# Layer 0 with its engines held to the traced order of instructions, a fourth e buffer, strip borders from ScalarE, and six groups ahead of the transposes

## The chip, the cores and the metric

The kernel runs on one core of a Trainium2 chip. The metric is device time in microseconds for one execution, and less is better. Times without a profiler come from several executions, of which the median is given. The profile comes from one execution of its own. Five engines matter: PE (TensorE, matrix products), DVE (VectorE), ACT (ScalarE), POOL (GpSimd) and SP (SyncE, which here issues nearly all DMAs). Each runs its own list of instructions from the front to the back, and engines wait for each other through semaphores.

## The reference

The input x has 4 images of 16 channels and 256 x 256 pixels. Two layers follow each other, and each adds its result to its input.

```
x = x + L0(_gn(x))     # _gn: normalization over 8 groups of 2 channels
x = x + L1(_gn(x))

# L0: a 3x3 convolution gives 16*25 logits for each pixel
out     = conv(x, conv_w) + conv_b
weights = softmax(out.reshape(N, C, 25, H, W), axis=2)
L0      = einsum('ncuij,ncuij->ncij', unfold5x5(x), weights)

# L1: a 3x3 convolution of silu(x) and of 8 cubic B-splines of x
L1      = einsum(silu(patches), base_w) + einsum(bspl(patches), spl_w) + bias
```

Layer 0 is the part that the change is about. For each pixel and channel it forms 25 exponentials, sums them, sums their products with the 5 x 5 neighbourhood, and divides the second sum by the first.

## The kernel before

The program is written with tiles and pools. A scheduler in the framework gives each engine its order of instructions: it goes by the order in which the code issued them (the traced order), but may put one ahead of another when it expects its operands earlier. Semaphores follow from the order that it settles on.

**Three stages.** The first reads x, gathers the statistics of the groups, builds the weights and normalizes image 0. The second is layer 0. It is written twice, with and without a shift of the logits, and a branch on `flag` picks one at run time; the traces here ran the one without. The third is layer 1. Nothing of one stage's instructions is mixed with those of the next.

**Layer 0's loops.** An image is cut into two halves of 128 rows, which lie on the 128 partitions, and each half into 8 strips of 32 columns: 64 strips in all for four images. A strip is worked in 8 groups of 4 columns (JG = 4), so there are 512 groups. The groups of a strip are counted here from 0 to 7. For one group:

- PE computes the 400 logits of each of 4 columns, in two products each: L544 with the operand am (from the scratch hst) and L548 with an (from hsl, the rounded value and its residue). The result lies in PSUM tiles lg of two columns, of which there are three.
- ACT takes the exponential of two columns at a time into `e[:, 0]` (L567).
- POOL multiplies all four columns by the neighbourhood u and writes `e[:, 1]` (L572).
- DVE sums both halves of e over the 25 neighbours into nd (L481).

The tile e is held from the first exponential to the end of the reduction. Its tag has `bufs=LAG + 2`, which is 3.

**The end of a strip.** The function `sums` runs one group late (LAG = 1): group k's reduction is issued after group k's successor has issued its product. With the last group of a strip it also calls `finish`: DVE takes the reciprocal of the denominators (L490), POOL multiplies by it (L491, "the division") and adds into xc, the held pixels of x (L494). With every fourth strip xc is complete: DVE takes bn_stats of it (L498), and a store of xc to x1s is queued.

**The next image.** While image b is worked, a generator `normalize(b + 1)` prepares the next one. The loop calls `next(ahead)` once in each group, so each `yield` in it stands for one group. For each four channels (q) and each half (h), ACT writes the normalized pixels in two arrangements: hsp (L205, rows with the borders of the strips, stored to hs and later read as u) and ht (L213, for transposing). The outer borders of hsp are zeroed by two memsets on POOL (L218, L219). Two groups later PE transposes ht (L237) into PSUM; after two more, ACT copies the result to tt (L244 to L246) and rounds it to hi (L248); after two more, DVE takes the residue lo = tt - hi (L252); after two more, SP stores tt, hi and lo to hst and hsl (L262, six DMAs). ACT's work on hsp and ht needs xp, the pixels of the next image, which SP loads (L184). Image 3 has no next one, so its strips are free of all this.

**SP's queue.** SP issues the loads of am and an (L439, L449; three buffers), u (L463; two), xc (L469), xp, and the stores. Each waits in its place for the buffer that it fills or for the data that it writes.

Of the kernel before, what the change touches and what calls it, by code (L numbers as in the profile page):

```python
# [9 lines left out]
F32 = mybir.dt.float32  # L10
# [20 lines left out]
def conv_preact_kernel(  # L31
# [12 lines left out]
    nc = tc.nc  # L44
    B, C, H, W = x.shape
    G = 8
    GC = C // G
    P = 128
    NH = H // P
    K = 5  # L50
    KK = K * K
    NL = C * KK
    PAD = K // 2
# [3 lines left out]
    SW = 32  # L57
    NST = W // SW
# [3 lines left out]
    JG = 4  # L62
    LAG = 1
    RP = P + 2
    CT = (W + 2) * RP
    QC = 4
# [9 lines left out]
    const = ctx.enter_context(tc.tile_pool(name="const", bufs=1))  # L76
# [87 lines left out]
    zero = const.tile([PAD * C, max(RP, NST * SP)], F32, name="zero")  # L164
    nc.vector.memset(zero, 0.0)

    def normalize(b, held=None):

        for e in (0, HP - PAD):
            for r in range(PAD):  # L170
                nc.sync.dma_start(
                    hs[b][:, e + r].rearrange("s c w -> c s w"),
                    zero[0:C, 0 : NST * SP].rearrange("c (s w) -> c s w", s=NST),
                )
        for h in range(NH):
            for w in (0, (W + 1) * RP):
                nc.sync.dma_start(hst[b][h][:, w : w + RP], zero[0:C, 0:RP])
                nc.sync.dma_start(
                    hsl[b][h][:, :, w : w + RP].rearrange("c t r -> (c t) r"), zero[:, 0:RP]
                )  # L180

        def load(q):
            for h in range(NH):
                nc.sync.dma_start(  # L184
                    xps[q % 2][h][:, :, PAD : PAD + W],
                    x[b, q * QC : (q + 1) * QC, h * P : (h + 1) * P, :].rearrange(
                        "c p w -> p c w"),
                )

        if held is None:  # L190
            load(0)
        yield
        for q in range(C // QC):
            if held is None and q + 1 < C // QC:
                load(q + 1)
            hts = []
            for h in range(NH):
                xp = xps[q % 2][h] if held is None else held[h][:, q * QC : (q + 1) * QC]
                hsp = prep.tile([P, NST, QC, SP], F32, name=f"hsp{b}_{q}_{h}", tag="hsp")
                ht = prep.tile([P, QW, W // QW, QC], F32, name=f"ht{b}_{q}_{h}", tag="ht")  # L200
                for k in range(QC // GC):
                    g = q * (QC // GC) + k
                    kc = slice(k * GC, (k + 1) * GC)
                    how = dict(scale=nrm[b][:, 0, g : g + 1], bias=nrm[b][:, 1, g : g + 1])
                    nc.scalar.activation(  # L205
                        hsp[:, :, kc, :].rearrange("p s c w -> p c s w"),
                        bass.AP(
                            tensor=xp.tensor, offset=xp.offset + k * GC * (W + 2 * PAD),
                            ap=[xp.ap[0], [W + 2 * PAD, GC], [SW, NST], [1, SP]],
                        ),  # L210
                        AF.Identity, **how,
                    )
                    nc.scalar.activation(  # L213
                        ht[:, :, :, kc].rearrange("p g w c -> p c w g"),
                        xp[:, kc, PAD : PAD + W].rearrange("p c (w g) -> p c w g", g=QW),
                        AF.Identity, **how,
                    )
                nc.gpsimd.memset(hsp[:, 0, :, 0:PAD], 0.0)  # L218
                nc.gpsimd.memset(hsp[:, NST - 1, :, PAD + SW :], 0.0)  # L219
                hts.append(ht)  # L220
                yield
                yield
                r0 = PAD + h * P
                nc.sync.dma_start(
                    hs[b][:, r0 : r0 + P, q * QC : (q + 1) * QC, :].rearrange(
                        "s r c w -> r s (c w)"),
                    hsp.rearrange("p s c w -> p s (c w)"),
                )
            yield
            yield  # L230
            for n, g0 in enumerate(range(0, QW, QG)):
                tt = tts[n % 2]
                tp = []
                for h in range(NH):
                    t = ptr.tile([P, QG, P], F32, name=f"tp{b}_{q}_{g0}_{h}", tag=f"tp{h}")
                    for k in range(QG):
                        nc.tensor.transpose(  # L237
                            t[:, k, :], hts[h][:, g0 + k].rearrange("p w c -> p (w c)"), ident
                        )
                    tp.append(t)  # L240
                yield
                yield
                for h in range(NH):
                    nc.scalar.copy(tt[:, h, :, 1 : 1 + P], tp[h])  # L244
                nc.scalar.copy(tt[:, 0, :, RP - 1 :], tp[1][:, :, 0:1])
                nc.scalar.copy(tt[:, 1, :, 0:1], tp[0][:, :, P - 1 :])  # L246
                hi = prep.tile([P, NH, QG, RP], F32R, name=f"hi{b}_{q}_{g0}", tag="hi")
                nc.scalar.copy(hi, tt)  # L248
                yield
                yield  # L250
                lo = prep.tile([P, NH, QG, RP], F32R, name=f"lo{b}_{q}_{g0}", tag="lo")
                nc.vector.tensor_sub(lo, tt, hi.bitcast(F32))  # L252
                yield
                yield
                for h in range(NH):

                    o = q * QC * CT + (1 + g0) * RP
                    for to, ti, t in ((hst, 0, tt), (hsl, 0, hi), (hsl, 1, lo)):
                        d = to[b][h]
                        m = 2 if to is hsl else 1  # L260
                        t = t if t.dtype == F32 else t.bitcast(F32)
                        nc.sync.dma_start(  # L262
                            bass.AP(
                                tensor=d.tensor,
                                offset=d.offset + q * QC * m * CT + ti * CT + (1 + g0) * RP,
                                ap=[[QW * RP, W // QW], [m * CT, QC], [1, QG * RP]],
                            ),
                            t[:, h].rearrange("p g r -> p (g r)"),
                        )
                yield  # L270


    with tc.tile_pool(name="pre", bufs=1) as pre, tc.tile_pool(
        name="xin", bufs=2
    ) as xin, tc.tile_pool(name="stat", bufs=2) as stat, tc.tile_pool(
        name="pstat", bufs=1, space=PSUM
# [51 lines left out]
        for b in range(B):  # L328
            st = stat.tile([P, G, NH * (GC if b == 0 else 1), 6], F32, name=f"st0_{b}", tag=f"st0{min(b, 1)}")
            for hf in range(NH):  # L330
                n = b * NH + hf
# [27 lines left out]
            if b == 0:  # L359
                ahead = normalize(0, held)  # L360
                next(ahead)
# [51 lines left out]
        for r in range(RT):  # L413
# [4 lines left out]
                ws[r * C : (r + 3) * C, :, r, :], wb1.rearrange("p (e o) -> p e o", e=3)  # L418
            )


    def layer0(shift):

        arm = "g" if shift else ""
        with tc.tile_pool(name=f"im{arm}", bufs=NIM) as imp, tc.tile_pool(
            name=f"l0{arm}", bufs=2
        ) as l0, tc.tile_pool(name=f"plog{arm}", bufs=3, space=PSUM) as plog:
# [38 lines left out]
            def load_xc(n):  # L466
                b, hf, s = strips[n]
                xc = l0.tile([P, C, CX], F32, name=f"xc_{n}{arm}", tag="xc")
                nc.sync.dma_start(  # L469
                    xc, x[b, :, hf * P : (hf + 1) * P, s * SW : s * SW + CX].rearrange(  # L470
                        "c p w -> p c w")
                )
                return xc
# [36 lines left out]
            for n, (b, hf, s) in enumerate(strips):  # L510
                if (hf, s) == (0, 0):
                    for _ in ahead:
                        pass
                    ahead = normalize(b + 1) if b + 1 < B else iter(())
                last = (hf, s) == (NH - 1, NST - 1)
# [8 lines left out]
                for j in range(0, SW, JG):  # L524
# [7 lines left out]
                    if j == SW // 2:  # L532
# [3 lines left out]
                            us.append(load_u(n + 1))  # L536
                        if s * SW % CX == SW and n + CX // SW - 1 < len(strips):
                            nxc = load_xc(n + CX // SW - 1)
                    e = l0.tile([P, 2, JG, K, C, K], F32, name=f"e_{n}_{j}{arm}", tag="e", bufs=LAG + 2)
                    for j1 in range(0, JG, 2):  # L540
                        lg = plog.tile([P, 2, 512], F32, name=f"lg_{n}_{j}_{j1}{arm}", tag="lg")
                        for i in range(2):
# [39 lines left out]
                sums()  # L582
            for o, i in stores:
                nc.sync.dma_start(o, i)

    fast = nc.values_load(
        flag[0:1, 0:1], min_val=0, max_val=1,
# [2 lines left out]
    with tc.If(fast > 0) as small_logits:  # L590
        layer0(False)
    with small_logits.Else():
        layer0(True)
# [3 lines left out]
    with tc.tile_pool(name="l1", bufs=2) as l1, tc.tile_pool(  # L597
        name="stat1", bufs=2
    ) as stat, tc.tile_pool(name="pstat1", bufs=1, space=PSUM) as pstat, tc.tile_pool(
        name="py", bufs=4, space=PSUM  # L600
# [106 lines left out]
        for n, (b, u) in enumerate(units):  # L707
# [3 lines left out]
            f, g = fb[n % 3], sl[n % 2]  # L711
# [89 lines left out]
```

## Time and profile before

| What | Value |
|---|---|
| median of 3 executions | 3744.49 us (3737.02 to 3744.62) |
| the profiled execution | 3743.14 us; span from first to last instruction 3741.2 us |
| mean granted TensorE clock | 0.937 |
| PE busy | 3136.8 us, 84% of the span |
| DVE busy | 3235.6 us, 86% |
| ACT busy | 2053.7 us, 55% |
| POOL busy | 2010.9 us, 54% |
| first and last reciprocal of layer 0 (DVE, L490) start | 204.74 and 2443.42 us |

The span is what the trace covers; the profiled execution's own time is 1.9 us longer, and it lies 1.4 us below the median. The page gives for each group of instructions its busy time, the mean duration of one, and the idle time of its engine just before, with what ended that idle time. The timeline lists single instructions, or runs of equal ones, with start and duration. Matmul ends are modelled, so a busy PE isn't PE at its peak.

### The profile page before, as it was taken

Reading aid. Unit: us, or ns where it says so; the run is one execution under the profiler, and the core shown is the slowest. Engines: PE = TensorE matmul, PEld = TensorE weight load, DVE = VectorE, ACT = ScalarE, POOL = GpSimd, SP = SyncE. Lnnn points to the kernel's source line nnn. Section 1 sums busy time; section 2 is a strip of 40 time slices with the busy share of each in tenths; the row PEclk is TensorE's granted clock in tenths of the full one; section 3 lists DMA queues with packets and bytes.
Section 4 is the critical chain, followed back from the end, with each engine's and each line's share of the span. In section 5 each row is a group of like instructions: output and inputs, shape, how many; then the busy total and the mean of one; then the engine's idle time right before and its main releaser. Section 6 shows DMA issues by size and latency. Waiting matters only on the chain. (4 is left out here: it accounts for less than half of the span.)

```text
span 3741.2 us, 34115 instructions
## 1 busy us (share of the span) xinstructions
PE 3136.8 (84%) x11824; PEld 1696.2 (45%) x11824; DVE 3235.6 (86%) x1627; ACT 2053.7 (55%) x1903; POOL 2010.9 (54%) x750
## 2 busy tenths in 40 slices
PE   1488888978779878779889889849998999998999
PEld 0255555555455545445555555513333433642333
DVE  9488899989899979899989989978788888888886
ACT  3454433454434355434334334358788888888884
POOL 1287888977889879789889989910000000000000
PEclk9999999989899989899989989969999999999999
DMA  7877575567576567665555555467687667667662
GB/s 238 254 213 205 164 198 162 148 177 214 161 202 173 152 185 200 189 194 162 162 157 160 145 156 161 109 134 168 165 177 176 171 172 176 168 168 176 169 168 78
DMA packets 361880, 646.08 MB, mean 173 GB/s; under 512 B 44402, under 2 KB 231140, under 8 KB 353508
## 3 DMA queue, kind: packets, MB, share of 16 engines
q1 hardware_dynamic: 351908, 626.90, 63.7%
q10 hardware_dynamic: 9792, 16.91, 1.4%
q8 instruction: 97, 1.59, 0.2%
q14 instruction: 83, 0.68, 0.1%
HBM read 522.34 MB, written 104.24 MB: 167 GB/s over the span
## 5 line engine op out<-in xcount | busy, mean ns | idle before, releaser
L544 PE MATMUL lg<-wm,am 128*128 128x400 f32 x4096 | 1758.9, 527 | 307.8 <-ACT e L567 283.0
L481 DVE TENSOR_REDUCE nd<-e 128x128 f32<-128x3200 f32 x512 | 1764.6, 3476 | 236.9 <-POOL e L572 153.5
L572 POOL TENSOR_TENSOR e<-e,u 128x1600 f32<-128x1600 f32 x512 | 1797.4, 3543 | 200.2 <-ACT e L567 170.5
L567 ACT ACTIVATE e<-lg 128x800 f32<-128x800 f32 x1024 | 838.1, 837 | 1331.5 <-DVE nd L481 664.3
L548 PE MATMUL lg<-wn,an 97*128 97x400 f32 x2048 | 1167.6, 605 | 0.0
L544 PEld LDWEIGHTS lg<-wm,am 128*128 128x128 f32 x4096 | 794.7, 200 | 670.2 <-ACT e L567 403.4
L742 PE MATMUL yp<-f,wt 128*64 128x512 f32 x4608 | 1031.3, 595 | 35.9 <-DVE f L640 22.6
L742 PEld LDWEIGHTS yp<-f,wt 128*64 128x64 f32 x4608 | 391.1, 136 | 653.2 <-issue 564.3
L680 POOL MEMSET sx<- 96x1024 f32 x8 | 8.5, 1065 | 1220.1 <-ACT sl L713 1213.9
L548 PEld LDWEIGHTS lg<-wn,an 97*128 97x128 f32 x2048 | 402.2, 196 | 324.0 <-issue 40.7
L634 ACT ACTIVATE r<-xt 128x2048 f32<-128x2048 f32 (+2 forms) x128 | 243.3, 1902 | 157.8 <-PE yp L742 32.3
L637 DVE TENSOR_SCALAR xt<-xt 128x2048 f32<-128x2048 f32 (+2 forms) x128 | 156.6, 1224 | 183.2 <-ACT s L635 183.2
L727 ACT ACTIVATE xt<-xt,qs 128x2048 f32<-128x2048 f32 (+2 forms) x128 | 264.9, 2081 | 57.7 <-DMA sx<-x1s 31.6
L638 DVE TENSOR_TENSOR s<-s,xt 128x2048 f32<-128x2048 f32 (+2 forms) x128 | 292.9, 2288 | 2.1
L639 DVE TENSOR_TENSOR s<-s,r 128x2048 f32<-128x2048 f32 (+2 forms) x128 | 292.5, 2285 | 2.6 <-ACT s L636 2.6
L640 DVE TENSOR_TENSOR f<-s,s 128x2048 f32<-128x2048 f32 (+2 forms) x128 | 288.7, 2286 | 0.8
L635 ACT ACTIVATE s<-xt 128x2048 f32<-128x2048 f32 (+2 forms) x128 | 242.5, 1895 | 2.7 <-DVE f L640 2.7
L636 ACT ACTIVATE s<-r 128x2048 f32<-128x2048 f32 (+2 forms) x128 | 242.7, 1896 | 0.0
L750 PE MATMUL yp<-sl,ws 96*64 96x512 f32 x768 | 204.8, 614 | 43.3 <-DMA sl<-zrow 27.3
L490 DVE RECIPROCAL nd<-nd 128x512 f32<-128x512 f32 x64 | 214.6, 3353 | 2.2
L237 PE MATMUL tp<-ident,ht 128*128 128x128 f32 x256 | 57.8, 385 | 124.1 <-ACT ht L213 81.0
L491 POOL TENSOR_TENSOR nd<-nd 128x512 f32<-128x512 f32 x64 | 81.8, 1278 | 143.2 <-DVE nd L490 142.2
(127 smaller groups left out, 843.0 us busy)
## 6 DMA issues: line engine op xcount, KB each, us to landing
xt<-x1s SPq DMA_DIRECT2D x56, 2048.0 KB
am<-hst SPq DMA_DIRECT2D x512, 194.6 KB
u<-hs SPq DMA_DIRECT2D x320, 288.0 KB
an<-hsl SPq DMA_DIRECT2D x512, 129.8 KB
am<-hst SPq DMA_DIRECT2D x256, 129.8 KB
sx<-x1s SPq DMA_DIRECT2D x224, 96.0 KB
hs<-hsp SPq DMA_DIRECT2D x32, 576.0 KB
hst<-tt SPq DMA_DIRECT2D x64, 260.0 KB
```

The costliest lines, as they stand in the source:

```text
L481: nc.vector.tensor_reduce(nd[:, :, j : j + JG, :], e.rearrange("p t j m c d -> p t j c m d"), AX.XY, ALU.add,)
L544: nc.tensor.matmul(lg[:, i, :NL], lhsT=am[:, o : o + P], rhs=wm.rearrange("p m c d -> p (m c d)"), start=True, stop=False,)
L548: nc.tensor.matmul(lg[:, i, :NL], lhsT=an[:, o : o + P], rhs=wn.rearrange("p m c d -> p (m c d)"), start=False, stop=True,)
L567: nc.scalar.activation(ev, lg[:, :, :NL], AF.Exp)
L572: nc.gpsimd.tensor_tensor(e[:, 1].rearrange("p j m c d -> p j (m c) d"), e[:, 0].rearrange("p j m c d -> p j (m c) d"), uv, ALU.mult,)
L634: nc.scalar.activation(r1, t, AF.Relu, bias=1.0, scale=-1.0)
L636: nc.scalar.activation(s1, r1, AF.Square, scale=2.0)
L638: nc.vector.tensor_mul(s2, s2, t)
L639: nc.vector.tensor_mul(s1, s1, r1)
L640: nc.vector.tensor_add(f, s2, s1)
L727: nc.scalar.activation(xt, xt, AF.Abs, scale=ra, bias=qa)
L742: nc.tensor.matmul(yp[t * M : (t + 1) * M], lhsT=wt[:, d, e].rearrange("p r o -> p (r o)"), rhs=f[:, t * RT + d : t * RT + d + 9 : 8, e : ...
```

## The change

Five things are edited.

- A new function `in_order` runs at the end of each `layer0`. It goes over all instructions that the stage has issued and ties each to the one issued before it on the same engine, without a semaphore. The scheduler can then no longer reorder them: PE, DVE, ACT, POOL and SP, with its DMAs, run layer 0 in the traced order. The other two stages are scheduled as before.
- The tag e has `LAG + 3` buffers, which is 4.
- The two memsets of the strip borders in hsp move from POOL to ACT, as copies of a zero tile `zpad` (128 x 8) that DVE fills once.
- `normalize` yields six times instead of twice between the rows and the first transpose. It counts 97 steps an image instead of 81; the loop drains what is left ahead of the last strip, at 120 groups.
- Line numbers move: L481 becomes L501, L490 L510, L491 L511, L494 L514, L498 L518, L567 L587, L572 L592, and in `normalize` L252 L255, L248 L251, L205 L208, L213 L216.

```diff
+    zpad = const.tile([P, QC, PAD], F32, name="zpad")
+    nc.vector.memset(zpad, 0.0)
...
-                nc.gpsimd.memset(hsp[:, 0, :, 0:PAD], 0.0)
-                nc.gpsimd.memset(hsp[:, NST - 1, :, PAD + SW :], 0.0)
+                nc.scalar.copy(hsp[:, 0, :, 0:PAD], zpad)
+                nc.scalar.copy(hsp[:, NST - 1, :, PAD + SW :], zpad)
...
-            yield
-            yield
+            for _ in range(6):
+                yield
             for n, g0 in enumerate(range(0, QW, QG)):
...
+    def in_order(first):
+
+        last = {}
+        for i in nc.cur_bb.bb.instructions[first:]:
+            if isinstance(i, (mybir.BassTileRelease, mybir.BassTilePoolBoundary)):
+                continue
+            if i.engine in last:
+                tc.add_manual_dep(
+                    i, last[i.engine],
+                    mybir.DependencyInfo(
+                        mybir.DependencyClass.NoSync, mybir.DependencyReason.DATA
+                    ),
+                    reason="order",
+                )
+            last[i.engine] = i.name
...
     def layer0(shift):
 
         arm = "g" if shift else ""
+        first = len(nc.cur_bb.bb.instructions)
...
-                    e = l0.tile([P, 2, JG, K, C, K], F32, name=f"e_{n}_{j}{arm}", tag="e", bufs=LAG + 2)
+                    e = l0.tile([P, 2, JG, K, C, K], F32, name=f"e_{n}_{j}{arm}", tag="e", bufs=LAG + 3)
...
             for o, i in stores:
                 nc.sync.dma_start(o, i)
+            in_order(first)
```

In the built program POOL's list in layer 0 before the change holds, at a strip's end, two products of the next strip ahead of the division in 44 of 64 strips, one ahead of it and one between it and the sum into xc in 4, and none in 16 (the last strip among them). After the change each strip but the last has one product of the next strip ahead of the division and the sum into xc, and all others behind. On DVE, bn_stats stood behind the first reduction of the next strip in 15 of its 16 places, and now stands ahead of it. The residue subtractions, which stood at various places of a strip, now stand between the seventh and the eighth reduction or between the sixth and the seventh, in turn.

## The prediction

> **What bounds the kernel now.** I read the page's shares first, then the slices, the waits, and last the timelines of DVE and POOL over single strips. DVE is busy for 86% of the span and is at 9 or 8 tenths in all slices from image 0's strips to about 2440 us; POOL works to the same point and then stops. So layer 0 is a DVE and POOL stage, and what counts in it is each moment in which DVE stands still. The groups (busy us, mean ns, idle us before and its releasers) say how long, and the waits (us, times, longest) add POOL's:
>
> ```profile
> L481 DVE TENSOR_REDUCE nd<-e 128x128 f32<-128x3200 f32 x512 | 1764.6, 3476 | 236.9 <-POOL e L572 153.5 <-POOL hsp L219 29.8 <-POOL hsp L218 26.3
> L572 POOL TENSOR_TENSOR e<-e,u 128x1600 f32<-128x1600 f32 x512 | 1797.4, 3543 | 200.2 <-ACT e L567 170.5 <-DMA u<-hs 29.2
> ```
>
> ```profile
> POOL nd L491 <- DVE nd L490: 142.2, 20, 10.3
> ```
>
> The reductions wait 237 us in all, mostly for POOL's products. The product waits for ScalarE's exponentials, and POOL's division step (L491) waits 20 times for the reciprocal. Two strips of image 3, where no other image is prepared, show in the timeline (start, us, line, count, idle before) what one strip end costs. First a strip whose POOL order puts the division and the sum into xc ahead of every product of the next strip:
>
> ```profile
> 2342.99 3.35 DVE L490 RECIPROCAL nd<-nd 128x512 f32<-128x512 f32 x1
> 2352.80 13.93 DVE L481 TENSOR_REDUCE nd<-e 128x128 f32<-128x3200 f32 x4 [6.45 <-POOL e L572]
> ...
> 2346.42 1.27 POOL L491 TENSOR_TENSOR nd<-nd 128x512 f32<-128x512 f32 x1 [7.26 <-DVE nd L490]
> 2347.77 1.52 POOL L494 TENSOR_TENSOR xc<-xc,nd 128x512 f32<-128x512 f32 x1
> 2349.25 13.95 POOL L572 TENSOR_TENSOR e<-e,u 128x1600 f32<-128x1600 f32 x4
> ```
>
> DVE ends the reciprocal at 2346.34 and has nothing to reduce for 6.45 us, because POOL must first do 1.27 + 1.52 and a product. Then a strip whose POOL order has two products of the next strip ahead of the division:
>
> ```profile
> 2384.69 27.44 DVE L481 TENSOR_REDUCE nd<-e 128x128 f32<-128x3200 f32 x8
> 2412.16 3.35 DVE L490 RECIPROCAL nd<-nd 128x512 f32<-128x512 f32 x1
> 2415.43 3.43 DVE L481 TENSOR_REDUCE nd<-e 128x128 f32<-128x3200 f32 x1
> ...
> 2387.69 27.89 POOL L572 TENSOR_TENSOR e<-e,u 128x1600 f32<-128x1600 f32 x8
> 2415.59 1.28 POOL L491 TENSOR_TENSOR nd<-nd 128x512 f32<-128x512 f32 x1
> ```
>
> No wait at all: eight reductions at 3.43 and a reciprocal, 30.74 us from start to start. In the program's order 44 strips have this form, 4 nearly so, 16 the first. From reciprocal to reciprocal, image 3 takes 537.5 us for 16 strips; images 1 and 2 take 585.7 and 580.3, since they prepare the next image. There the order hurts otherwise: ScalarE does a batch of normalizing while POOL starves:
>
> ```profile
> 776.94 3.52 POOL L572 TENSOR_TENSOR e<-e,u 128x1600 f32<-128x1600 f32 x1 [12.77 <-ACT e L567]
> 768.78 1.24 DVE L252 TENSOR_TENSOR lo<-tt,hi 128x1040 fp32r<-128x1040 f32 x1 [2.65 <-ACT hi L248]
> 835.49 4.39 DVE L252 TENSOR_TENSOR lo<-tt,hi 128x1040 fp32r<-128x1040 f32 x1
> 831.79 11.47 POOL L572 TENSOR_TENSOR e<-e,u 128x1600 f32<-128x1600 f32 x3
> ```
>
> The last three lines matter below: the residue subtraction lo takes 1.24 us while POOL is still, and 4.39 when it comes just after a POOL product began.
>
> **What the Trainium skill says.** "SBUF — State Buffer", section "SBUF: two separate sides": a DVE operation with two SBUF inputs and a GpSimd operation that reads SBUF share a port pair under an exclusive lock; whichever starts first keeps it for the whole instruction and the other fully blocks. The trace agrees: 4.39 against 1.24. The one-input reduction isn't hit (3.43 beside products). "Perfetto Trace Analysis", section "Tensor Engine Instruction (MATMUL, LD_WEIGHTS)": ACT, DVE and GPSIMD are strict FIFO. So a waiting division holds every product queued behind it; the 6.45 us above agrees. "TensorE: Matmul & The Clock Gate", section "What's actually happening": an idle window drops the clock to half. The trace agrees: PE idles at 744 to 748 and is granted 0.50 from 748 to 752.
>
> **The change, part by part.**
>
> *The order on POOL.* As traced, group k issues its product, then sums() of group k-1. At a strip's end this gives POOL: product 0 of the next strip, division, sum into xc, product 1, always. One product ahead, in all strips. The period follows from the rows above. Let T be the reciprocal's end. The division starts at T+0.08, and the next product at T+2.91 (2346.34 to 2349.25). Seven products follow at a pitch of 3.48 (13.95/4) and the last of the strip ends at T+27.3. Its reduction (3.49) and the reciprocal (3.35) with two gaps of 0.03 give **34.2 us**. Check: the first strip above took 38.43 with one product more (3.48) and a wait for ScalarE of 0.71: 38.43 - 3.48 - 0.71 = 34.24. DVE idles 3.0 in it. So the strips of the first kind gain about 4, and the plain ones among the 44 lose about 3.4.
>
> *The order on DVE: bn_stats.* Every fourth strip, the statistics (2.69) now stand directly behind the reciprocal and wait for POOL's sum into xc, T+2.95; before, a reduction stood between. All of the next strip's reductions queue behind it. A two-ahead strip with statistics takes 33.09 now (2342.99 - 2309.90); plus 2.95: **36.0**.
>
> *The order on DVE: lo.* 24 subtractions, eight for each of three images, stand after the sixth or seventh reduction of a strip. 18 fall into plain strips. There DVE follows POOL by 0.03 us, so each reduction ends about when POOL begins its next product, by the rows some 0.08 after it. I take lo as blocked for that product: 4.4 each, 79 us. Bounds: 1.24, if lo gets the lock first, and 4.5, the longest seen. Six fall into strips with statistics, where DVE lags POOL by 2.6 and the rest of the product is about 1.2: 2.4 each, 14.5 us.
>
> Sum from the first to the last reciprocal: 48 x 34.2 + 15 x 36.0 + 79 + 14.5 = 1641.6 + 540 + 93.5 = 2275. The profile has 2443.42 - 204.74 = 2238.7. So **+36**.
>
> *The order on ScalarE, the fourth e buffer, the zero copies, six yields.* Batches of normalizing are now 2 x (0.86 + 1.27) and two copies of about 0.19 (row L246's size, 194 ns), 4.6 us, with two groups of exponentials between. With four buffers, exponentials may start when the reduction four groups back ends, 7.0 before POOL needs them; they take 1.7, so 5.2 is to spare and a batch fits. It falls after groups 1 and 3 of a strip, where the pause at the strip's end adds slack. The waits on hsp (56 us), on ScalarE (170) and on PE's transposes go; they are already missing from the 34.2, so nothing is added for them. If the cover fails, a batch costs up to its 4.6. The memsets leave POOL: 64 x 0.107 = 7 us, mostly beside waits. Six groups instead of two before the transposes let ht be finished first; 97 steps still fit into an image's 120 groups.
>
> *SP.* Its order hardly moves. The six stores of hst and hsl now wait for lo, with the next am loads behind; these have three buffers, and PE needs the data some 6 us after T, while the stores are out by about T-3. I cost it at nothing; bound 0 to 10 us a store, 24 of them. At an image's start ScalarE waits for xp: issued at 738.75 now, landed by about 748. The strip with statistics is there and gives slack: 0, up to 8 for each of two images.
>
> *The start.* Image 0 loses about 20 us now to one big batch; as ordered I get the first reciprocal about 3 us earlier. Ahead of layer 0, 16 sets of copies go to ScalarE beside the DMA issues; layer 1 keeps its order: 0, within 3.
>
> Total 36 - 3 = +33 on the profiled execution of 3743.1 (span 3741.2): 3776. It lies 1.4 below the median of 3744.5, so the forecast is about **3776**.
>
> **The rivals.**
> - *lo wins the lock.* DVE asks only some 0.08 us after POOL's product begins; if the lock is taken later than that, 18 x 3.15 = 57 us vanish: 3719, **faster**. For: a strip in image 1 at 482.00 had lo wait only for the running product's end (1.76). Against: at 336.65 it came 0.12 after a product's start and took 4.50. It decides at half of the 18: below nine blocked, the total gains.
> - *In-order ScalarE or SP uncovered.* 12 of 24 batches at 4.6 and two late xp at 8 would add 70: 3846; with a third of this, 3800. For: waits of 12.77 now. Against: buffer four and the strip's pause.
> - *All waits vanish, DVE alone sets the pace.* 64 x 30.74 + 16 x 2.69 + 24 x 1.24 = 2040, 199 less: 3545. Against: product 1 stands behind the division, and four buffers can't change that.
> - *The order isn't kept.* The program's order on all five engines shows it kept; no chance given.
>
> **How the numbers follow.** About 0.2% (7.5 us) is what a measurement can tell from no change. Main case, slower: 0.64, with 3765 to 3790. lo wins: 0.17. Some lo blocked, within 0.2%: 0.05. Uncovered ScalarE or SP: 0.11, slower. More waits gone: 0.03. Faster 0.20, same 0.05, slower 0.75. The range 3718 to 3800 takes in the main case, both ends of lo and the mildest of the uncovered cases.
>
> **What would show it.** Right: reciprocals 34.2 apart in image 3 and 36.0 where the statistics stand; POOL's division (L511) waiting some 3.4 us at all strips, over 200 us; L501 waiting about 3 for L592 in each plain strip; lo (L255) at a mean near 4; no wait for hsp, few for ScalarE. Wrong: image 3 at 31 a strip (rival three); lo near 1.3 (rival one); products waiting for ScalarE or PE for DMA (rival two).

## The result, and the profile after

The change made the kernel slower: 3783.19 us (median of 4, 3773.07 to 3787.29) against 3742.04 us of the kernel before on the same chip, a ratio of 1.0108 with the interval 1.0083 to 1.0132. The forecast was 3776 from a base of 3744.5. The profiled execution has a span of 3785.3 us, 44.1 more than before; the medians lie 41.2 apart, since the profiled execution of after was the longest of its four.

The groups of the page of after (columns as before: busy us, mean ns, idle us before and its releasers):

```profile
L501 DVE TENSOR_REDUCE nd<-e 128x128 f32<-128x3200 f32 x512 | 1769.7, 3477 | 194.2 <-POOL e L592 168.2
L592 POOL TENSOR_TENSOR e<-e,u 128x1600 f32<-128x1600 f32 x512 | 1792.5, 3543 | 56.7 <-ACT e L587 56.7
L511 POOL TENSOR_TENSOR nd<-nd 128x512 f32<-128x512 f32 x64 | 81.7, 1276 | 357.7 <-DVE nd L510 357.7
```

The waits that the old order caused are smaller or gone: the products wait 57 us for exponentials instead of 170 and no longer for u, and the reductions no longer wait for the memsets (56 us before). Another is far larger. POOL stands 358 us ahead of its divisions, at every strip end, where before it stood 142 us at 20 of them. The waits of DVE between 200 and 2490 us name the two that count (total us, times, longest):

```profile
DVE nd L501 <- POOL e L592: 150.2, 48, 3.2
DVE st L518 <- POOL xc L514: 44.8, 15, 3.0
```

48 plain strips at 3.13 us and 15 strips with statistics at 2.99 us: 195 us of DVE standing still, in an order that is the same everywhere. The timelines of two strips of image 3 (start, us, line, count, idle before), first DVE and then POOL:

```profile
2320.73 3.35 DVE L510 RECIPROCAL nd<-nd 128x512 f32<-128x512 f32 x1
2324.00 3.43 DVE L501 TENSOR_REDUCE nd<-e 128x128 f32<-128x3200 f32 x1
2330.57 24.36 DVE L501 TENSOR_REDUCE nd<-e 128x128 f32<-128x3200 f32 x7 [3.14 <-POOL e L592]
2354.97 3.35 DVE L510 RECIPROCAL nd<-nd 128x512 f32<-128x512 f32 x1
2361.30 2.71 DVE L518 BATCH_NORM_STATS2 st<-xc 128x6 f32<-128x256 f32 x8 [2.98 <-POOL xc L514]
2363.93 27.22 DVE L501 TENSOR_REDUCE nd<-e 128x128 f32<-128x3200 f32 x8
2391.18 3.35 DVE L510 RECIPROCAL nd<-nd 128x512 f32<-128x512 f32 x1
```

```profile
2324.16 1.28 POOL L511 TENSOR_TENSOR nd<-nd 128x512 f32<-128x512 f32 x1 [3.50 <-DVE nd L510]
2325.53 1.54 POOL L514 TENSOR_TENSOR xc<-xc,nd 128x512 f32<-128x512 f32 x1
2327.01 27.88 POOL L592 TENSOR_TENSOR e<-e,u 128x1600 f32<-128x1600 f32 x8
```

In the first strip DVE reduces group 0, and then waits 3.14 us, because POOL's next product starts only at 2327.01, after division and sum. The period, from reciprocal to reciprocal, of the plain strip is 34.24 us, that of the strip with statistics 36.21.

### The profile page after: what moved, and what is told of

The parts are those of the page before. It is cut to its first block, busy times and chain, and to the rows that moved or that the text cites. A ratio compares the mean times of both kernels' runs of the same rounds, so it can differ in the third digit from the quotient of the medians.

```text
span 3785.3 us, 33969 instructions
## 1 busy us (share of the span) xinstructions
PE 3175.3 (84%) x11824; PEld 1672.8 (44%) x11824; DVE 3295.2 (87%) x1628; ACT 2049.7 (54%) x1967; POOL 2003.7 (53%) x686
## 5 line engine op out<-in xcount | busy, mean ns | idle before, releaser
L564 PE MATMUL lg<-wm,am 128*128 128x400 f32 x4096 | 1857.9, 536 | 391.3 <-ACT e L587 367.8
L501 DVE TENSOR_REDUCE nd<-e 128x128 f32<-128x3200 f32 x512 | 1769.7, 3477 | 194.2 <-POOL e L592 168.2
L592 POOL TENSOR_TENSOR e<-e,u 128x1600 f32<-128x1600 f32 x512 | 1792.5, 3543 | 56.7 <-ACT e L587 56.7
L587 ACT ACTIVATE e<-lg 128x800 f32<-128x800 f32 x1024 | 826.2, 836 | 1364.3 <-DVE nd L501 1072.7
L568 PE MATMUL lg<-wn,an 97*128 97x400 f32 x2048 | 1419.5, 693 | 0.0
L763 PEld LDWEIGHTS yp<-f,wt 128*64 128x64 f32 x4608 | 361.5, 136 | 682.3 <-issue 645.7
L568 PEld LDWEIGHTS lg<-wn,an 97*128 97x128 f32 x2048 | 412.2, 201 | 337.1 <-issue 62.9
L511 POOL TENSOR_TENSOR nd<-nd 128x512 f32<-128x512 f32 x64 | 81.7, 1276 | 357.7 <-DVE nd L510 357.7
L510 DVE RECIPROCAL nd<-nd 128x512 f32<-128x512 f32 x64 | 214.6, 3353 | 2.2
L771 PEld LDWEIGHTS yp<-sl,ws 96*64 96x64 f32 x768 | 64.5, 139 | 155.1 <-issue 99.1
```

The costliest lines, as they stand in the source:

```text
L501: nc.vector.tensor_reduce(nd[:, :, j : j + JG, :], e.rearrange("p t j m c d -> p t j c m d"), AX.XY, ALU.add,)
L564: nc.tensor.matmul(lg[:, i, :NL], lhsT=am[:, o : o + P], rhs=wm.rearrange("p m c d -> p (m c d)"), start=True, stop=False,)
L568: nc.tensor.matmul(lg[:, i, :NL], lhsT=an[:, o : o + P], rhs=wn.rearrange("p m c d -> p (m c d)"), start=False, stop=True,)
L587: nc.scalar.activation(ev, lg[:, :, :NL], AF.Exp)
L592: nc.gpsimd.tensor_tensor(e[:, 1].rearrange("p j m c d -> p j (m c) d"), e[:, 0].rearrange("p j m c d -> p j (m c) d"), uv, ALU.mult,)
L763: nc.tensor.matmul(yp[t * M : (t + 1) * M], lhsT=wt[:, d, e].rearrange("p r o -> p (r o)"), rhs=f[:, t * RT + d : t * RT + d + 9 : 8, e : ...
```

## The experiments

The table gives the mean time between reciprocals, by kind of strip, from the traces: 30 plain strips without a residue subtraction lo, 18 with one, 9 with statistics, 6 with statistics and lo. Ratios are against the kernel before on the same chip, with their intervals. The runs were on several chips, where the kernel before took 3735.37 to 3744.12 us, so compare ratios and periods rather than medians.

| Kernel | median us | ratio | plain | plain, lo | statistics | statistics, lo |
|---|---|---|---|---|---|---|
| after | 3783.19 | 1.0108 (1.0083 to 1.0132) | 34.23 | 39.41 | 36.22 | 38.63 |
| e1, two products ahead | 3593.23 | 0.9627 (0.9596 to 0.9659) | 30.77 | 36.73 | 33.09 | 36.91 |
| e2, lo at the strip's start | 3709.51 | 0.9923 (0.9901 to 0.9944) | 34.23 | 35.10 | 36.22 | 38.05 |
| e3, three e buffers | 3790.32 | 1.0136 (1.0110 to 1.0161) | 34.23 | 39.22 | 36.53 | 40.21 |
| e4, before and the order | 3790.76 | 1.0145 (1.0121 to 1.0168) | 34.26 | 38.77 | 36.64 | 39.61 |
| e5, lo with one input | 3707.65 | 0.9919 (0.9901 to 0.9938) | 34.23 | 35.24 | 36.22 | 37.36 |
| e6, statistics later | 3769.78 | 1.0094 (1.0077 to 1.0111) | 34.22 | 39.02 | 34.23 | 39.22 |
| e7, e1 and e2 | 3508.08 | 0.9386 (0.9364 to 0.9407) | 30.92 | 32.46 | 33.09 | 34.30 |
| e9, borders on POOL | 3789.98 | 1.0123 (1.0103 to 1.0143) | 34.28 | 38.84 | 36.22 | 39.20 |
| e10, two groups | 3783.76 | 1.0092 (1.0066 to 1.0117) | 34.23 | 38.79 | 36.22 | 39.21 |

e8 keeps the scheduler's order, so its strips are of other kinds; it is told of below.

**e1: is it the one product ahead of the division?** Here there are two. All that POOL does at a strip's end, and the statistics, move one group later:

```diff
-            waiting, stores = [], []
+            waiting, stores, late = [], [], []
...
                 nc.vector.reciprocal(nd[:, 0], nd[:, 0])
+                late.append(partial(finish_pool, n, nd, xc))
+
+            def finish_pool(n, nd, xc):
+                b, hf, s = strips[n]
                 nc.gpsimd.tensor_mul(nd[:, 1], nd[:, 1], nd[:, 0])
...
+                    due = late[:]
+                    late.clear()
                     if len(waiting) > LAG:
                         sums()
+                    for d in due:
+                        d()
```

> The changed kernel, but POOL's division, its sum into xc and the statistics are issued one group later, behind the next group's product and reduction; all else stays. Theory (one product ahead of the division sets the strip's period): plain strips go from 34.2 to 30.7 us between reciprocals, those with statistics from 36.2 to 33.1, so 48 x 3.5 + 15 x 3.1 = 214 us less, and lo costs what it did: about 3570, 3530 to 3600. DVE no longer waits for POOL's products in plain strips. Rival (PE or ScalarE is nearly as tight and takes over): half of the gain, about 3675, with POOL waiting for exponentials. Rival (the division isn't the cause): within 10 of 3783.

3593.23 us, a ratio of 0.9627. Plain strips fell to 30.77 and those with statistics to 33.09. The group of reductions from 200 to 2490 us, with 150 us of waiting for POOL in after:

```profile
L501 DVE TENSOR_REDUCE nd<-e 128x128 f32<-128x3200 f32 x504 | 1726.6, 3473 | 0.1
```

The wait is gone, so the place of the division, and of the sum behind it, in POOL's list caused it. PE and ScalarE did not take over: POOL waits 1.9 us for exponentials in these strips. The gain fell short of the expected 214 because lo grew dearer, its 24 taking 5.60 us in the mean instead of 4.67: its strips now lose 18 x 5.96 + 6 x 3.82 = 130 us, against 18 x 5.18 + 6 x 2.41 = 108 in after.

**e2: where lo stands.** Only the yields of `normalize` change, so that lo falls directly behind the reciprocal, or behind the statistics where there are any:

```diff
-            for _ in range(6):
+            for _ in range(7):
                 yield
...
                 nc.vector.tensor_sub(lo, tt, hi.bitcast(F32))
                 yield
-                yield
+                if n == 0:
+                    yield
...
-                yield
+                if n == 0:
+                    yield
+                    yield
```

> The changed kernel with other numbers of yields in normalize: the residue subtraction lo stands directly behind a strip's reciprocal (or its statistics) instead of behind the sixth or seventh reduction; the transposes and copies move by one to three groups. Theory (lo is blocked by a product on POOL, and now falls where POOL begins its division and DVE would idle 3 us): 18 times about 1.25 and 6 times about 2.1 a strip, 35 us, instead of the 108 that the reciprocals show: about 3710; lo's mean duration 1.3 to 2.6. Rival (lo costs the same wherever it stands): within 10 of 3783. Rival (moved transposes or copies come late): above 3783.

3709.51 us, as the theory had it (3710). The timelines of DVE and POOL at one such strip end:

```profile
233.46 3.35 DVE L513 RECIPROCAL nd<-nd 128x512 f32<-128x512 f32 x1
236.72 1.18 DVE L255 TENSOR_TENSOR lo<-tt,hi 128x1040 fp32r<-128x1040 f32 x1
237.82 3.47 DVE L504 TENSOR_REDUCE nd<-e 128x128 f32<-128x3200 f32 x1
244.14 24.38 DVE L504 TENSOR_REDUCE nd<-e 128x128 f32<-128x3200 f32 x7 [2.85 <-POOL e L595]
```

```profile
236.89 2.15 POOL L514 TENSOR_TENSOR nd<-nd 128x512 f32<-128x512 f32 x1 [3.51 <-DVE nd L513]
239.11 1.51 POOL L517 TENSOR_TENSOR xc<-xc,nd 128x512 f32<-128x512 f32 x1
```

lo comes first, takes 1.18, and now the division is the one that is held: 2.15 instead of 1.28. DVE would have idled there anyway, so the strip loses only 0.87.

**e5: is it the shared port pair?** lo is written at the same places by an operation that reads tt alone. The kernel leaves out the subtraction of hi, so lo is no residue here:

```diff
-                nc.vector.tensor_sub(lo, tt, hi.bitcast(F32))
+                nc.vector.tensor_reduce(
+                    lo.bitcast(F32), tt.unsqueeze(4), AX.X, ALU.add
+                )
```

> The changed kernel with lo written at the same places by a one-input reduction over an axis of length 1 of tt; the subtraction of hi is left out, so the residues are wrong. Theory (lo waits only because its two inputs need the port pair that POOL's products hold): each takes about 1.2 us, 24 x 1.2 = 29 us instead of 108, total about 3705, plain strips with lo at 35.4. Rival (DVE waits at this place for something else, the landing of hi or the order): durations stay at 4.6 and the total at 3783.

3707.65 us, near the expected 3705. The group of lo, first of after and then of e5:

```profile
L255 DVE TENSOR_TENSOR lo<-tt,hi 128x1040 fp32r<-128x1040 f32 x24 | 112.0, 4668 | 0.0
```

```profile
L255 DVE TENSOR_REDUCE lo<-tt 128x1040 f32<-128x1040 f32 x24 | 29.4, 1225 | 0.0
```

At the same places, in the same order, ahead of the same stores, it takes 1.225 us instead of 4.668. The operation is another one too, but the subtraction itself takes only 1.18 where no product runs beside it (e2). So what costs is a second SBUF input beside POOL's products, as the Trainium skill, "SBUF — State Buffer", section "SBUF: two separate sides", says of the lock. A late hi is excluded as the cause in after as well: neither group shows idle time ahead of it.

**e6: the statistics alone.** Their loop and the store move into a function that is called one group later, as in e1; POOL's order stays that of after.

```diff
                 if w0 + SW == CX:
+                    late.append(partial(stats, n, xc))
+
+            def stats(n, xc):
+                    b, hf, s = strips[n]
                     k = hf * (W // CX) + s * SW // CX
...
```

> The changed kernel with the statistics alone issued one group later, behind the first reduction of the next strip; POOL's order stays. Theory (the statistics wait for POOL's sum into xc while DVE could reduce, and DVE idles there anyway): strips with statistics go from 36.2 to 34.2, 15 x 2.0 = 30 us less; but lo in those six strips loses DVE's lag of 2.6 and is blocked longer, up to 12 us more: 3750 to 3770. Rival (the wait is hidden): within 8 of 3783.

3769.78 us, at the expected range's upper end. DVE at one such strip end, where 0.51 of the wait is left:

```profile
2336.28 3.35 DVE L510 RECIPROCAL nd<-nd 128x512 f32<-128x512 f32 x1
2339.55 3.43 DVE L501 TENSOR_REDUCE nd<-e 128x128 f32<-128x3200 f32 x1
2342.90 2.69 DVE L522 BATCH_NORM_STATS2 st<-xc 128x6 f32<-128x256 f32 x8
2346.10 24.35 DVE L501 TENSOR_REDUCE nd<-e 128x128 f32<-128x3200 f32 x7 [0.51 <-POOL e L596]
```

Strips with statistics take 34.23, like plain ones: the 2.7 us of statistics fit into DVE's idle 3. With lo they rose from 38.63 to 39.22. Its ratio's interval overlaps that of after, so here the periods are the evidence, not the median.

**e3, e9 and e10: the other three parts taken back one at a time.**

```diff
# e3
-                    e = l0.tile([P, 2, JG, K, C, K], F32, name=f"e_{n}_{j}{arm}", tag="e", bufs=LAG + 3)
+                    e = l0.tile([P, 2, JG, K, C, K], F32, name=f"e_{n}_{j}{arm}", tag="e", bufs=LAG + 2)
# e9
-                nc.scalar.copy(hsp[:, 0, :, 0:PAD], zpad)
-                nc.scalar.copy(hsp[:, NST - 1, :, PAD + SW :], zpad)
+                nc.gpsimd.memset(hsp[:, 0, :, 0:PAD], 0.0)
+                nc.gpsimd.memset(hsp[:, NST - 1, :, PAD + SW :], 0.0)
# e10
-            for _ in range(6):
+            for _ in range(2):
```

> The changed kernel with three e buffers again. The prediction counted 5.2 us to spare for the exponentials with four buffers; with three it is about 1.7. Theory (the batches stand where the strip's end gives slack, so the order alone is enough): same strips, 34.2 to 35, total 3780 to 3815. Rival (a normalizing batch of 4.6 us is uncovered with three): 24 batches at about 3, 3850 or more, POOL waiting over 100 us for exponentials.

> The changed kernel with the strip borders set by POOL's memsets again. Theory (with four buffers ScalarE's batch is over before POOL comes to the memsets, so they cost their own 0.1 each, 48 in layer 0): 0 to 6 us more, 3780 to 3792. Rival (in the traced order POOL waits there for ScalarE, as the kernel before showed for 29 us, and the next product behind it): 24 places at 1 to 3, 3810 or more.

> The changed kernel with two groups between rows and transposes again. The preparation of an image is then 80 groups instead of 96, and lo stands behind the second, third, sixth and seventh reductions. Theory (PE comes to the transposes after ScalarE's batch either way, and lo is blocked at all these places): 3770 to 3800. Rival (PE waits for ht at the transposes and its products come late): 3805 or more, with PE waiting for ScalarE's L216.

3790.32, 3789.98 and 3783.76 us; all three intervals overlap that of after, so none of the three parts is worth an amount that these runs can tell. With three buffers POOL waits 28 us for exponentials in the strips (38 times, at most 1.8), where after shows none. The strips with statistics grew by 0.3 and, with lo, by 1.6, which is 12 us in all; in five of the six that hold a lo, the lo took 3.9 to 4.6 instead of 2.4 to 2.5. The rival of uncovered batches (3850) is out.

**e4: the order alone**, put into the kernel before by `in_order` and its call:

```diff
+        first = len(nc.cur_bb.bb.instructions)
...
+            in_order(first)
```

> The kernel before with the order alone: three e buffers, borders set on POOL, two groups between rows and transposes. lo then stands behind the second, third, sixth or seventh reduction. Theory (the order is the whole cause of the loss, through one product ahead and blocked lo): reciprocals 34.2 apart in image 3, total 3765 to 3810. Rival (the other parts are needed to make the order bearable): over 3820, with POOL waiting at the borders' memsets for ScalarE or PE at the transposes.

3790.76 us, a ratio of 1.0145 (1.0121 to 1.0168), with 34.26 for the plain strip. The order alone makes the whole loss.

**e8: the fourth buffer alone**, in the kernel before, where the scheduler still orders:

```diff
-                    e = l0.tile([P, 2, JG, K, C, K], F32, name=f"e_{n}_{j}{arm}", tag="e", bufs=LAG + 2)
+                    e = l0.tile([P, 2, JG, K, C, K], F32, name=f"e_{n}_{j}{arm}", tag="e", bufs=LAG + 3)
```

> The kernel before with a fourth e buffer alone; the scheduler's order is the same in all but details. Theory (POOL's 170 us of waiting for exponentials came from buffers as much as from batches): reductions wait for about half of their 237 us, total 3640 to 3710, with image 3 at 525 to 535. Rival (the scheduler's batches of 15 us outlast any fourth buffer): 3725 to 3745.

3682.99 us, a ratio of 0.9861 (0.9844 to 0.9877), faster. The groups of its page:

```profile
L481 DVE TENSOR_REDUCE nd<-e 128x128 f32<-128x3200 f32 x512 | 1762.2, 3475 | 187.5 <-POOL e L572 149.2
L572 POOL TENSOR_TENSOR e<-e,u 128x1600 f32<-128x1600 f32 x512 | 1798.7, 3553 | 107.2 <-ACT e L567 107.2
```

The products wait 107 us for exponentials instead of 170, the reductions 187 instead of 237. They did not fall to about half, as expected; the total is in the range. Image 3 takes 529.2 us instead of 537.5, images 1 and 2 566 and 567 instead of 586 and 580. POOL's list has the same number of products ahead of each division as before, strip by strip, so the gain is not a better order there. The buffer is worth 1.4% in the scheduler's order, most of it in images that hold batches, and in the traced order at most some 12 us (e3), since exponentials come in time anyway. Beside a kernel with this buffer the order therefore costs more than the result shows: 1.0108 against 0.9861, about 2.5%.

**e7: both gains together.** e1's edit on e2's kernel.

> Both edits of the first two experiments together: POOL's end work and the statistics one group later, lo directly behind the reciprocal. In the first experiment lo still cost 18 x 6.0 + 6 x 3.8 = 130 us. Theory (the two costs are separate, and lo at the division costs about 1.2): plain 30.8, with lo 32.0, with statistics 33.1: 101 less than the first experiment, about 3492. Rival (POOL has only 0.5 us of slack in a two-ahead strip, so lo's lock on the division comes through twice, or PE's 27.5 a strip and its cold starts take over): 3520 or more.

3508.08 us, a ratio of 0.9386 (0.9364 to 0.9407): faster than both kernels by over 6%. lo isn't blocked in e7: it takes 1177, 1230 and 1250 ns at the shortest, in the median and at the longest. The total lies between theory (3492) and rival (3520). Most strips have the theory's periods, but eight plain ones stand at 32.9 to 34.8. PE's waits from 200 to 2220 us show what could delay them:

```profile
PE lg L571 <- ACT e L594: 113.9, 64, 5.2
PE lg L571 <- DMA am<-hst: 50.8, 14, 6.4
```

PE waits 14 times for am, and each of the eight has one of these waits, of 3.8 us or more, in it or within 1.1 us ahead of it. e2, with the same places of lo and of the stores, shows this wait too (44.1 us, 13 times), but its strips have slack and don't lengthen. In the strip from 261.53 SP stood at a store of lo until 266.07, 14.0 us, and issued the next loads of am at 269.91; PE then waited for am until 278.07. That such stores ahead of am in SP's list cause the waits is my reading; no run took it apart.

## Why the prediction was right

It named the right mechanism, and the sum came out 11 us short of the span's 44. That it came so near is in part luck: from the first to the last reciprocal it was 19 short, and 8 of these were made up by an earlier start and by scatter behind the last reciprocal. By its own steps:

| Step | predicted | measured |
|---|---|---|
| plain strips | 48 x 34.2 = 1641.6 | 48 x 34.23 = 1643 |
| strips with statistics | 15 x 36.0 = 540 | 15 x 36.22 = 543 |
| lo in plain strips | 18 x 4.4 = 79 | 18 x 5.18 = 93 |
| lo with statistics | 6 x 2.4 = 14.5 | 6 x 2.41 = 14.5 |
| first to last reciprocal | 2275, +36 | 2294.1, +55.4 |
| first reciprocal | 3 earlier | 5.0 earlier (199.76) |
| after the last reciprocal | 0 | 6.4 less |

- **POOL's order: right.** One product ahead gave 34.2 and a wait of 3.0; the trace has 34.23 and 3.13, and e1 removes both. POOL's wait ahead of the division was put at 3.4 a strip and over 200 us. It is 3.5 in plain strips, more where statistics or lo stretch the strip, and 358 in all.
- **The statistics: right**, shown by e6.
- **lo: the mechanism right, the size short.** The step "I take lo as blocked for that product: 4.4 each" with the bound "4.5, the longest seen" is the mis-sized term. 14 of the 18 are blocked for one product (4.6), but four for two (8.1), and these four lengthen their strips by 7.8 instead of 4.4, which is nearly all of the 14 us that the term fell short. One of these, on DVE and then on POOL:

```profile
600.13 8.10 DVE L255 TENSOR_TENSOR lo<-tt,hi 128x1040 fp32r<-128x1040 f32 x1
```

```profile
589.68 17.45 POOL L592 TENSOR_TENSOR e<-e,u 128x1600 f32<-128x1600 f32 x5
```

  POOL's five products follow each other until 607.13 without a gap, and lo, which asked at 600.13 as the fourth began, ends only at 608.23. I had taken it that a waiting subtraction gets the ports at the end of the product that it waits for. The bound from the longest of 24 in the kernel before was no bound. The place was misread a little too: the 18 began between 0.02 us ahead of a product's start and 0.03 behind it, not 0.08 behind it, and those that began ahead were blocked as well, so these recorded starts don't tell who comes first.
- **The rival "lo wins the lock": out for this kernel.** None of the 24 took less than 2.4. e5, where no lo is held, shows about what it would have given: a ratio of 0.9919, against 3719 / 3744.5 = 0.9932 in the prediction. It was no idle rival: one lo in e3 and two in e4 that began within 0.01 us of a product's start took 1.23, and the product took 4.62 or 4.63 instead.
- **The fourth buffer, the borders, the six groups at nothing: right** as far as e3, e9 and e10 can tell. That all waits for exponentials vanish is right too: after 200 us POOL waits for nothing but the division.
- **SP at nothing: right for after**, where PE's waits in layer 0 show no DMA of weight.
- **The start and the end.** The first reciprocal came 5.0 earlier. The stretch behind the last one was 6.4 shorter in after; over the eleven traces besides before it lies between 1285.8 and 1303.3 with the same code in layer 1, so I take this as scatter and no effect.

## What to carry to other kernels

Holding engines to the written order repeats every wait of that order in each round of the loop: read for each engine what stands behind its waiting instruction, and count how much work its partner has in hand when it starts to wait. Here the place of a strip's end work (two products ahead of the division instead of one, with the statistics moved along) was worth 5% and turned a loss of 1.1% into a gain of 3.7%. The two-input DVE operation beside POOL's unbroken products belonged where POOL waits. Almost seven microseconds of waiting can hide in the duration of one instruction (8.10 instead of 1.2), where no column of idle time shows them.

## What the runs showed of the hardware

A waiting two-input DVE operation can lose the ports several times in a row, as these traces show. In plain strips lo's durations cluster: 1.2 where nothing holds it, 4.62, 8.10, and in e1 11.57 and 11.58. Each step is 3.47 or 3.48, as long as one of POOL's products in a row (27.88 for eight). What decides how many go by stays open: in after, subtractions that began within 0.03 us of a product's start were blocked now for one product and now for two, three in e3 and e4 went ahead of the product (1.23), and in the kernel before one that asked some 3.4 us ahead of the product's end (336.65) was served at that end. A one-input reduction of the same 1040 elements was not held once in e5: 24 times between 1.221 and 1.228 us.
